# A convolution and attention-plus-scan kernel: the projection's convolution spread over the whole step, halo rows kept in one tile, and GpSimd's output products taken in pairs

## The chip, the cores and the metric

One NeuronCore of a Trainium2 chip runs the whole program. The metric is device time in microseconds for one execution. The kernel before took 16,462.36 us, the median of three runs (16,461.45 to 16,478.73 us).

## What is computed

The input `x` is 2 images of 256 x 256 positions with 128 channels, in fp32. Two layers follow, each with a residual and each on a group-normalised input `_gn` (32 groups of 4 channels, statistics over the whole image).

Layer 0 is an attention along one image axis. It takes some 15% of the time and the change does not touch it.

Layer 1 is a state-space layer. Cut to what matters:

```python
xi, z = split(x @ in_proj_w.T)               # 256 channels each
xi = silu(depthwise_conv3x3(xi) + conv_b)    # over the image
xs = xi.reshape(B, 256, L)                   # L = 65536 positions
dts, Bs, Cs = split(x_proj_w @ xs)           # 8, 16 and 16 rows
delta = softplus(dt_w @ dts + dt_b)          # 256 x L
# for every channel d (256) and state n (16), along L:
h = exp(delta * A[d, n]) * h + delta * xs * Bs[n]
y[d] = sum_n Cs[n] * h[d, n] + Ds[d] * xs[d]
y = layernorm(y) * silu(z)
out = x + y @ out_proj_w.T
```

The recurrence is sequential over the 65,536 positions of an image, for 256 x 16 = 4,096 pairs of a channel and a state.

## The kernel before

**Tiling.** Layer 1 goes through each image in steps of R = 4 rows, T = 1,024 positions: 64 steps an image, 128 in all. In a step the 4,096 pairs of channel and state are NU = 32 *units* of 128 partitions each, a partition being one channel with one of SR = 4 states of a group. A unit's number t gives the step k, the half of the channels h (2), the group of states m (4) and the quarter q of the half (4), in that order, q fastest (`unit`, line 907).

**What a unit is.** Five operations on tiles of 128 x 1024:
- `drive` (line 948, GpSimd): hb = du x B, from two tiles that DMA has replicated, `du_r` and `bb`
- `decay` (line 940, ScalarE): da = exp(delta x A), into PSUM. There are two da tiles, for even and for odd units
- `scan` (line 954, VectorE): the recurrence. For most units it writes its result over da; for a *pooled* unit over hb
- `product` (line 966): yc = h x C, from the replicated tile `cc`. VectorE does it, for pooled units GpSimd (line 970)
- `remember` (line 961, ScalarE): keeps the last column as the state for the next step

`add_up` (line 975, TensorE) then sums the products of four units into y, in 8 matmuls (16 records in the profile). At h's first group it starts y with Ds x xs (line 984). `pooled` (line 937) names 9 of 32 units by their number in the step: `POOLED = (4, 7, 10, 13, 16, 19, 24, 26, 31)`.

**What else a step holds.** `project(k)` (line 606) makes what step k needs: rows loaded and turned (`load`, `turn`), normalised into `xn` (`normalise`), the convolution as nine matmuls with shifted views for each of four output blocks (`conv`, two records a matmul in the profile), z (`gate`), then x_proj (`states`), dt_w (`size`), softplus and du = delta x xs (`times`, GpSimd). Three long ScalarE operations belong to it: `silu_xs`, `softplus`, `silu_z`, each 128 x 2048, each with a table of its own, so that a table is loaded ahead of it and exp's again ahead of the next decay. Its convolution needs a halo: the last two rows of xn are kept by GpSimd in a tile `keep` and copied into the next xn by GpSimd. All the projection's matmul results go through one PSUM buffer, tag "p": one must be evacuated by ScalarE before the next begins. `finish_row` (line 804) does the layernorm, gate and output projection for a row of the step before, nine pieces in nine slots; its `gated` (line 872) is a VectorE product of 128 x 512. Its results go through one PSUM buffer too, tag "f".

**The order.** It is written out by hand for TensorE, ScalarE, VectorE and GpSimd (`manual_schedule`, line 1017): one slot for each unit. In slot t the program issues, in this order, `drive(t + 2)`, the GpSimd product of unit t - 1 if pooled, `decay(t + 1)`, `scan(t)` and VectorE's product of t, `add_up` for units t - 5 to t - 2 if t - 5 is a multiple of four, then the pieces of projections and rows that `at(slot, piece)` has put into the slot, in the order of their entry, and at last `remember(t)`. Each engine runs its part of that list in order. In a projection of step k the slots count from `base` = 32 (k - 2), so it runs one to two steps ahead: convolution and z in slots 2 to 18 after base, silu_xs in 21, states and sizes in 22 to 28, softplus in 29, times in 31 and 32, silu_z in 33. DMAs are issued from SyncE, whose order is not written out; `fetch(t + 6)` (line 916) asks for a unit's replicated tiles six slots ahead. `bb` and `cc` have three buffers, `delta_r` and `du_r` five each.

Of the kernel before, what the change touches and what calls it, by code (L numbers as in the profile page):

```python
# [8 lines left out]
F32 = mybir.dt.float32  # L9
AF = mybir.ActivationFunctionType  # L10
ALU = mybir.AluOpType
# [4 lines left out]
P = 128  # L16
# [5 lines left out]
def attn_then_ssm_kernel(  # L22
# [557 lines left out]
    NU = NCG * NSG  # L580
    NM = NQ * NSG

    POOLED = (4, 7, 10, 13, 16, 19, 24, 26, 31)
    s1 = ctx.enter_context(tc.tile_pool(name="s1", bufs=1))
    s2 = ctx.enter_context(tc.tile_pool(name="s2", bufs=2))
    s3 = ctx.enter_context(tc.tile_pool(name="s3", bufs=3))
    s5 = ctx.enter_context(tc.tile_pool(name="s5", bufs=5))
    s8 = ctx.enter_context(tc.tile_pool(name="s8", bufs=8))
    ps_d = ctx.enter_context(tc.tile_pool(name="ps_d", bufs=1, space=PSUM))
    ps_y = ctx.enter_context(tc.tile_pool(name="ps_y", bufs=1, space=PSUM))  # L590
    ps_p = ctx.enter_context(tc.tile_pool(name="ps_p", bufs=1, space=PSUM))
# [5 lines left out]

    slots = {}

    def at(t, piece, *args):  # L600
        slots.setdefault(t, []).append((piece, args))

    halo = {}
    given = {}

    def project(k):
# [19 lines left out]
                )  # L626

        def begin():


            xn = o["xn"] = s1.tile([P, R + 2, WP], F32, name="xn")
            nc.gpsimd.memset(xn[:, :, 0:1], 0.0)
            nc.gpsimd.memset(xn[:, :, WP - 1 : WP], 0.0)
            if s == 0:
                nc.gpsimd.memset(xn[:, 0, :], 0.0)
                turn("first", 0, 1)
                normalise(1, 1)
            else:
                nc.gpsimd.tensor_copy(xn[:, 0:2, 1 : W + 1], halo.pop(k - 1))
            if n < R:  # L640
                nc.gpsimd.memset(xn[:, 2 + n, :], 0.0)

        def turn(src, r, m):
            t_ps = o["t"] = ps_p.tile([P, RB, W], F32, name="t_ps", tag="p")
# [5 lines left out]

        def normalise(to, m):
            nc.scalar.activation(
                o["xn"][:, to : to + m, 1 : W + 1],
                o["t"][:, 0:m, :],
                AF.Identity,
                bias=sh,
                scale=rs,
            )

        def keep():  # L660
            if s + 1 < NSTEP:
                halo[k] = s2.tile([P, 2, W], F32, name="keep")
                nc.gpsimd.tensor_copy(halo[k], o["xn"][:, R : R + 2, 1 : W + 1])

        def conv(h, i, dy):
            if dy == 0:
                o["u"] = ps_p.tile([P, RB, W], F32, name="u_ps", tag="p")
            for dx in range(3):
                nc.tensor.matmul(  # L669
                    o["u"],  # L670
                    w_tap[:, h, 3 * dy + dx, :],
                    o["xn"][:, i * RB + dy : i * RB + dy + RB, dx : dx + W],
                    start=(dy == 0 and dx == 0),
                    stop=(dy == 2 and dx == 2),
                )

        def conv_out(h, i):
            if (h, i) == (0, 0):
                o["xs"] = s1.tile([P, NH, T], F32, name="xs")
            nc.scalar.activation(  # L680
                o["xs"][:, h, i * TB : (i + 1) * TB],
                o["u"].rearrange("p r w -> p (r w)"),
                AF.Identity,
                bias=cb_c[:, h : h + 1],
            )
# [6 lines left out]
        def gate(h, i):  # L692
            o["z"] = ps_p.tile([P, RB, W], F32, name="z_ps", tag="p")
            nc.tensor.matmul(
                o["z"],
                w_z[:, h, :],
                o["xn"][:, 1 + i * RB : 1 + (i + 1) * RB, 1 : W + 1],
                start=True,
                stop=True,
            )  # L700
# [62 lines left out]
            nc.gpsimd.tensor_tensor(du, o["delta"][:, h, :], du, ALU.mult)  # L763
            nc.sync.dma_start(out=v["du"][h], in_=du)

        at(base - 14, load)
        at(base - 4, begin)
        for r in range(0, n, RB):
            at(base - 3 + r, turn, "raw", r, min(RB, n - r))
            at(base - 2 + r, normalise, 2 + r, min(RB, n - r))  # L770
        at(base + 1, keep)
        t = base + 2
        for h in range(NH):
            for i in range(NB):
                for dy in range(3):
                    at(t + dy, conv, h, i, dy)
                at(t + 3, conv_out, h, i)
                at(t + 3, gate, h, i)
                at(t + 4, gate_out, h, i)
                t += 4  # L780
        t = base + 21
        at(t, silu_xs)
        at(t + 1, states, 0)
        at(t + 2, states_out, 0)
        at(t + 2, states, 1)
        at(t + 3, states_out, 1)
        t += 3
        for h in range(NH):
            for i in range(NB):
                at(t, size, h, i)  # L790
                at(t + 1, size_out, h, i)
                t += 1
        at(base + 29, softplus)
        at(base + 31, times, 0)
        at(base + NU, times, 1)
        at(base + NU + 1, silu_z)

    def finish(k):

        b, s = steps[k]  # L800
        for r in range(R):
            finish_row(k, b, R * s + r, r * W, (k + 1) * NU + 3 + r * (NU // R))

    def finish_row(k, b, row, t0, a):
        o = {}

        def fetch():
            o["xres"] = s2.tile([P, WT, C], F32, name="xres")
            nc.sync.dma_start(
                out=o["xres"], in_=x1[b][row].rearrange("(t p) c -> p t c", p=P)  # L810
            )
            o["szr"] = s2.tile([P, NH, W], F32, name="szr")
            nc.sync.dma_start(
                out=o["szr"], in_=given[k]["sz"][:, :, t0 : t0 + W].rearrange("h p t -> p h t")
            )
# [78 lines left out]
                in_=ob,  # L894
            )

        at(a - 3, fetch)
        for i, piece in enumerate(
            (turn, stats, scales, norm, back, affine, gated, mix, leave)
        ):  # L900
            at(a + i, piece)

    states_of = {}
    ys = {}
# [2 lines left out]
    def unit(t):  # L907

        k, i = divmod(t, NU)
        h, i = divmod(i, NM)  # L910
        m, q = divmod(i, NQ)
        return k, h, m, q
# [3 lines left out]
    def fetch(t):  # L916
        k, h, m, q = unit(t)
        v = given[k]
        if q == 0:

            for name, row in (("bb", m * SR), ("cc", NS + m * SR)):
                tl = repeats[name, k, h, m] = s3.tile([P, T], F32, name=name)
                nc.sync.dma_start(
                    out=tl, in_=v["bc"][row : row + SR, :].partition_broadcast(CQ)
                )
        if m == 0:

            for name in ("delta", "du"):
                tl = spreads[name, k, h, q] = s5.tile([P, T], F32, name=f"{name}_r")
                nc.sync.dma_start(  # L930
                    out=tl,
                    in_=v[name][h, q * CQ : (q + 1) * CQ, :]
                    .unsqueeze(1)
                    .to_broadcast([CQ, SR, T]),
                )

    def pooled(t):
        return t % NU in POOLED

    def decay(t):  # L940
        k, h, m, q = unit(t)
# [4 lines left out]
        )  # L946

    def drive(t):
        k, h, m, q = unit(t)
        hb = s5.tile([P, T], F32, name="hb")  # L950
        units[t] = {"hb": hb}
        nc.gpsimd.tensor_tensor(hb, spreads["du", k, h, q], repeats["bb", k, h, m], ALU.mult)  # L952

    def scan(t):
        k, h, m, q = unit(t)
# [10 lines left out]
    def product(t):  # L966
        k, h, m, q = unit(t)
        u = units[t]
        u["yc"] = s8.tile([P, T], F32, name="yc")
        eng = nc.gpsimd if pooled(t) else nc.vector  # L970
        eng.tensor_tensor(u["yc"], u["h"], repeats["cc", k, h, m], ALU.mult)  # L971

    outs = {}

# [26 lines left out]
    def y_out(t):  # L1001
        k, h, _, _ = unit(t)
        ys[k, h] = s2.tile([P, T], F32, name=f"ys{h}")
        nc.scalar.copy(ys[k, h], outs["y"])
# [12 lines left out]
    with tc.manual_schedule(engines=engines):  # L1017
        for t in range(min(slots), max(slots) + 1):
            if 0 <= t + AHEAD < end:
                fetch(t + AHEAD)  # L1020
            if 0 <= t < end and t % (NU * NSTEP) == 0:
                st = s1.tile([P, NCG, NSG], F32, name="state")
                nc.gpsimd.memset(st, 0.0)
                states_of[steps[t // NU][0]] = st
            if 0 <= t + 2 < end:
                drive(t + 2)
            if 0 <= t - 1 < end and pooled(t - 1):
                product(t - 1)
            if 0 <= t + 1 < end:
                decay(t + 1)  # L1030
            if 0 <= t < end:
                scan(t)
                if not pooled(t):
                    product(t)
            if 0 <= t - 5 < end and (t - 5) % NQ == 0:
                add_up(t - 5)
            if 0 <= t - 6 < end and unit(t - 6)[2:] == (NSG - 1, 0):
                y_out(t - 6)
            for piece, args in slots.pop(t, ()):
                piece(*args)  # L1040
            if 0 <= t < end:
                remember(t)

# [36 lines left out]
```

## Time and profile before

| | |
|---|---|
| median of three runs | 16,462.36 us |
| the profiled execution | 16,465.48 us |
| its span, first to last instruction | 16,463.4 us |
| first scan starts | 2,690.5 us into the span |
| last scan ends | 16,405.2 us |
| the 128 steps between | 13,714.6 us, 107.15 us each |

The profile's page gives, engine by engine, the busy time and its share, and then the costliest groups of instructions: the source line, the engine, the operation, output and input tiles with partitions x elements, the count, the busy time in us, the mean of one instruction in ns, and the idle time of that engine just ahead of them with what ended it. A timeline has the start in us, the length in us, engine, line, operation and tiles, and in brackets the idle time ahead of it with its releaser. PE is TensorE, DVE VectorE, ACT ScalarE, POOL GpSimd, SP SyncE. Consecutive instructions of an engine overlap a little where neither waits, so the cost of one is the distance between starts.

### The profile page before, as it was taken

The page shows a single profiled execution, that of the slowest core. Times are in us where ns is not written, and L with a number is a line of the kernel's source. Part 1 is how long each engine was busy: PE and PEld are TensorE (multiplying, and loading weights), DVE is VectorE, ACT ScalarE, POOL GpSimd, SP SyncE. Part 2 cuts the span into 40 slices and gives each one's busy share as a digit, 9 for nine tenths or more (in the row PEclk, how much of TensorE's full clock was granted, in tenths as well). Part 3 has the DMA queues.
Part 4 walks back from the last instruction along what each step waited for, and adds up shares of the span by engine and source line. Part 5 has one row for each costly group of instructions (what it writes and reads, how often), then busy time and mean ns, then how long its engine had stood idle before and what let it go on. Part 6 is the DMA issues. An engine that isn't in the chain of part 4 may idle for free. (4 is left out here: it accounts for less than half of the span.)

```text
span 16463.4 us, 177150 instructions
## 1 busy us (share of the span) xinstructions
PE 13687.6 (83%) x55353; PEld 6810.9 (41%) x55353; DVE 14807.3 (90%) x12607; ACT 11039.0 (67%) x19870; POOL 13686.2 (83%) x7308
## 2 busy tenths in 40 slices
PE   6999997888888888888888888888888888888886
PEld 5777873333333333333333333333333333333333
DVE  7665555999999999999999999999999999999998
ACT  3555554677776677766777766777776767777665
POOL 0111114999999999999999999999999999999998
PEclk9999998888899888889998889999889998889997
DMA  4322224666666666666666666666666666666665
GB/s 186 131 86 88 82 83 146 232 234 230 232 234 230 233 232 232 233 229 232 233 233 231 233 228 232 232 235 231 230 229 230 234 234 231 233 230 234 230 231 171
DMA packets 1428932, 3452.05 MB, mean 210 GB/s; under 512 B 119784, under 2 KB 711184, under 8 KB 1407504
## 3 DMA queue, kind: packets, MB, share of 16 engines
q1 hardware_dynamic: 1427984, 3440.73, 60.6%
q8 instruction: 434, 7.11, 0.2%
q14 instruction: 514, 4.21, 0.1%
HBM read 2752.41 MB, written 687.88 MB: 209 GB/s over the span
## 5 line engine op out<-in xcount | busy, mean ns | idle before, releaser
L952 POOL TENSOR_TENSOR hb<-du_r,bb 128x1024 f32<-128x1024 f32 x4096 | 9575.1, 2363 | 0.0
L959 DVE TENSOR_TENSOR_SCAN da<-da,state,hb 128x1024 f32<-128x1024 f32 x2944 | 6903.2, 2345 | 327.8 <-ACT da L944 321.8
L944 ACT ACTIVATE da<-delta_r,a_neg 128x1024 f32<-128x1024 f32 x4096 | 4576.8, 1117 | 88.6 <-ACT state L964 0.8
L669 PE MATMUL u_ps<-xn,w_tap 128*128 128x512 f32 x9216 | 4230.3, 604 | 181.8 <-ACT state L964 168.2
L971 DVE TENSOR_TENSOR yc<-da,cc 128x1024 f32<-128x1024 f32 x2944 | 3604.7, 1224 | 254.9 <-DVE da L959 5.0
L971 POOL TENSOR_TENSOR yc<-hb,cc 128x1024 f32<-128x1024 f32 x1152 | 2719.6, 2361 | 203.0 <-issue 166.6
L959 DVE TENSOR_TENSOR_SCAN hb<-da,state,hb 128x1024 f32<-128x1024 f32 x1152 | 2697.3, 2341 | 72.6 <-ACT da L944 72.5
L991 PE MATMUL y<-yc,sel 128*32 128x512 f32 x16384 | 2527.4, 682 | 236.6 <-POOL yc L971 229.9
L669 PEld LDWEIGHTS u_ps<-xn,w_tap 128*128 128x128 f32 x9216 | 1718.3, 193 | 2190.5 <-issue 1781.4
L428 POOL TENSOR_TENSOR x1g<-xc,bo_all 128x512 f32<-128x512 f32 x256 | 315.9, 1273 | 1841.6 <-DVE stats L477 1839.7
L964 ACT COPY state<-da 128x1 f32<-128x1 f32 x2944 | 459.6, 156 | 1527.6 <-DVE yc L971 1525.8
L991 PEld LDWEIGHTS y<-yc,sel 128*32 128x32 f32 x16384 | 496.8, 116 | 1937.6 <-issue 1117.5
L821 PE MATMUL yt<-centre,ys 128*128 128x256 f32 x4096 | 1072.2, 407 | 218.4 <-ACT ob L891 217.4
L680 ACT ACTIVATE xs<-u_ps,cb_c 128x512 f32<-128x512 f32 x512 | 351.9, 687 | 1257.3 <-PE u_ps L669 977.9
L856 PE MATMUL yd<-ident,yn 128*128 128x128 f32 x2048 | 403.4, 331 | 906.5 <-ACT yn L845 877.5
L378 ACT ACTIVATE e<-s_ps,nmx 128x256 f32<-128x256 f32 x1024 | 477.6, 476 | 967.3 <-DVE nmx L369 955.1
L717 PE MATMUL xd_ps<-xs,w_xp 128*64 128x512 f32 x1024 | 683.5, 805 | 479.6 <-ACT state L964 374.8
L821 PEld LDWEIGHTS yt<-centre,ys 128*128 128x128 f32 x4096 | 794.2, 200 | 602.7 <-ACT ob L891 379.2
L735 PE MATMUL dt_ps<-xd,w_dt 8*128 8x512 f32 x1024 | 693.6, 761 | 270.7 <-ACT xd L730 263.9
L856 PEld LDWEIGHTS yd<-ident,yn 128*128 128x128 f32 x2048 | 291.2, 169 | 1263.8 <-ACT yn L845 916.2
L345 DVE TENSOR_TENSOR v<-v_ps,bv_all 128x512 f32<-128x512 f32 x256 | 177.0, 691 | 592.0 <-PE v_ps L338 592.0
L881 PEld LDWEIGHTS o_ps<-w_out,yg 128*128 128x128 f32 x4096 | 626.8, 219 | 41.4
(131 smaller groups left out, 17289.1 us busy)
## 6 DMA issues: line engine op xcount, KB each, us to landing
bb<-bc_d SPq DMA_DIRECT2D x1024, 512.0 KB, 4.2
cc<-bc_d SPq DMA_DIRECT2D x1024, 512.0 KB, 5.3
delta_r<-delta_d SPq DMA_DIRECT2D x1024, 512.0 KB, 5.6
du_r<-du_d SPq DMA_DIRECT2D x1024, 512.0 KB, 4.1
xs_d<-xs SPq DMA_DIRECT2D x128, 1024.0 KB, 6.9
xr<-xs_d SPq DMA_DIRECT2D x256, 512.0 KB, 7.2
delta_d<-delta SPq DMA_DIRECT2D x128, 1024.0 KB, 6.9
du_d<-xs SPq DMA_DIRECT2D x256, 512.0 KB, 3.2
```

Source lines behind the costliest of these rows:

```text
L378: nc.scalar.activation(e[:, i, :], o["s", r][:, i, :], AF.Exp, bias=o["nmx", r][:, i : i + 1], scale=SM, accum_out=o["den"][:, r, i : i + 1],)
L669: nc.tensor.matmul(o["u"], w_tap[:, h, 3 * dy + dx, :], o["xn"][:, i * RB + dy : i * RB + dy + RB, dx : dx + W], start=(dy == 0 and dx == ...
L717: nc.tensor.matmul(o["xd_ps"], w_xp[:, h, :], o["xs"][:, h, i * TB : (i + 1) * TB], start=(h == 0), stop=(h == NH - 1),)
L735: nc.tensor.matmul(o["dt"], w_dt[:, h, :], o["xd"][0:DR, i * TB : (i + 1) * TB], start=True, stop=True,)
L821: nc.tensor.matmul(o["yt"][:, j, :], ys[k, h][:, t0 + j * P : t0 + (j + 1) * P], centre[:, (1 - h) * P : (1 - h) * P + DI], start=(h == 0) ...
L856: nc.tensor.transpose(o["yd"][:, h, j * P : (j + 1) * P], o["yn"][:, j, h * P : (h + 1) * P], ident,)
L881: nc.tensor.matmul(o["o"][:, j, :], o["yg"][:, h, j * P : (j + 1) * P], w_out[:, h, :], start=False, stop=(j == WT - 1 and h == NH - 1),)
L944: nc.scalar.activation(da, spreads["delta", k, h, q], AF.Exp, scale=a_neg[:, g, m : m + 1])
L952: nc.gpsimd.tensor_tensor(hb, spreads["du", k, h, q], repeats["bb", k, h, m], ALU.mult)
L959: nc.vector.tensor_tensor_scan(u["h"], u["da"], u["hb"], st, ALU.mult, ALU.add)
L971: eng.tensor_tensor(u["yc"], u["h"], repeats["cc", k, h, m], ALU.mult)
L991: nc.tensor.matmul(y[q * CQ : (q + 1) * CQ, cols], sel, units[t + q]["yc"][:, cols], start=False, stop=(m == NSG - 1),)
```

## The change

- **Pooled units come in pairs.** `POOLED = (6, 10, 14, 22, 30)` names even units; each stands for itself and the next: 10 of 32. GpSimd's product is one instruction over both (128 x 2 x 1024), with `cc` broadcast over the pair, in the slot after the second unit.
- **`drive` works by pairs for all units**: one GpSimd instruction in each odd slot t, for units t + 3 and t + 4, with `bb` broadcast over the pair. `hb` has three pair buffers (before: five single ones), `du_r` three pair buffers (five single ones), `yc` four pair buffers (eight single ones).
- `bb` and `cc` have two buffers in place of three; `xs` has two in place of one; `xres` and `szr` one in place of two, asked for one slot ahead of the row's first piece in place of three.
- **One `xn` tile stays for the whole layer.** It is zeroed once; ScalarE copies its last two rows to its first two at a step's beginning. GpSimd's two edge memsets, `keep` and the copy back go.
- **The convolution is spread**: its four blocks begin in slots 3, 11, 19 and 27 after base, with 2, 2, 3 and 2 of the nine taps in the block's slots 0, 1, 2 and 4, and are evacuated in slot 5 of the block. z goes to slots 2, 24, 25 and 26; silu_z to 29, silu_xs to 37, states to 40 and 41, sizes to 42, 48, 49 and 50, softplus to 53, times to 55 and 56. In the numbers of the running step silu_xs stands in slot 5, softplus in 21, silu_z in 29.
- Rows begin in slot 7 of the step in place of 3, so VectorE's `gated` falls into slots 5, 13, 21 and 29 (before: 1, 9, 17, 25). `add_up` and `y_out` come one slot later.
- In a slot, pieces without TensorE work are issued ahead of those with it.

```diff
-    POOLED = (4, 7, 10, 13, 16, 19, 24, 26, 31)
+    POOLED = (6, 10, 14, 22, 30)
...
+    xn = s1.tile([P, R + 2, WP], F32, name="xn")
+    nc.gpsimd.memset(xn, 0.0)
...
-                nc.gpsimd.tensor_copy(xn[:, 0:2, 1 : W + 1], halo.pop(k - 1))
+                nc.scalar.copy(xn[:, 0:2, 1 : W + 1], xn[:, R : R + 2, 1 : W + 1])
...
+        CY = NU // 4
+        for c in range(4):
+            h, i = divmod(c, NB)
+            t = base + c * CY + 3
+            for dt, taps in ((0, (0, 1)), (1, (2, 3)), (2, (4, 5, 6)), (4, (7, 8))):
+                at(t + dt, conv, h, i, taps, pe=True)
+            at(t + 5, conv_out, h, i)
+        for t, (h, i) in ((2, (0, 0)), (24, (0, 1)), (25, (1, 0)), (26, (1, 1))):
+            at(base + t, gate, h, i, pe=True)
+            at(base + t + 1, gate_out, h, i)
+        at(base + 29, silu_z)
+        at(base + 37, silu_xs)
+        for t, i in ((40, 0), (41, 1)):
+            at(base + t, states, i, pe=True)
+            at(base + t + 1, states_out, i)
+        for t, (h, i) in ((42, (0, 0)), (48, (1, 0)), (49, (0, 1)), (50, (1, 1))):
+            at(base + t, size, h, i, pe=True)
+            at(base + t + 1, size_out, h, i)
+        at(base + 53, softplus)
+        at(base + 55, times, 0)
+        at(base + 56, times, 1)
...
-                tl = repeats[name, k, h, m] = s3.tile([P, T], F32, name=name)
+                tl = repeats[name, k, h, m] = s2.tile([P, T], F32, name=name)
...
     def pooled(t):
-        return t % NU in POOLED
+        return t % NU - t % 2 in POOLED
...
     def drive(t):
+
         k, h, m, q = unit(t)
-        hb = s5.tile([P, T], F32, name="hb")
-        units[t] = {"hb": hb}
-        nc.gpsimd.tensor_tensor(hb, spreads["du", k, h, q], repeats["bb", k, h, m], ALU.mult)
+        hb = s3.tile([P, 2, T], F32, name="hb")
+        units[t] = {"pair": hb, "hb": hb[:, 0, :]}
+        units[t + 1] = {"hb": hb[:, 1, :]}
+        nc.gpsimd.tensor_tensor(
+            hb,
+            spreads["pair", k, h, q],
+            repeats["bb", k, h, m].unsqueeze(1).to_broadcast([P, 2, T]),
+            ALU.mult,
+        )
...
+    def products(t):
+
+        k, h, m, q = unit(t)
+        hb = units[t]["pair"]
+        yc = s4.tile([P, 2, T], F32, name="yc")
+        for i in range(2):
+            units[t + i]["yc"] = yc[:, i, :]
+        nc.gpsimd.tensor_tensor(
+            yc, hb, repeats["cc", k, h, m].unsqueeze(1).to_broadcast([P, 2, T]), ALU.mult
+        )
...
-            if 0 <= t + 2 < end:
-                drive(t + 2)
-            if 0 <= t - 1 < end and pooled(t - 1):
-                product(t - 1)
+            if 0 <= t + 3 < end and t % 2:
+                drive(t + 3)
+            if 0 <= t - 2 < end and t % 2 == 0 and pooled(t - 2):
+                products(t - 2)
...
-            if 0 <= t - 5 < end and (t - 5) % NQ == 0:
-                add_up(t - 5)
+            if 0 <= t - 6 < end and (t - 6) % NQ == 0:
+                add_up(t - 6)
```

## The prediction

> **What bounds the kernel now.** I read the page's shares and costliest groups first, then the waits of VectorE, the starts of all 4,096 scans in VectorE's timeline, and then two steps closely.
>
> ```profile
> PE 13687.6 (83%) x55353; PEld 6810.9 (41%) x55353; DVE 14807.3 (90%) x12607; ACT 11039.0 (67%) x19870; POOL 13686.2 (83%) x7308
> L952 POOL TENSOR_TENSOR hb<-du_r,bb 128x1024 f32<-128x1024 f32 x4096 | 9575.1, 2363 | 0.0
> L959 DVE TENSOR_TENSOR_SCAN da<-da,state,hb 128x1024 f32<-128x1024 f32 x2944 | 6903.2, 2345 | 327.8 <-ACT da L944 321.8
> L971 DVE TENSOR_TENSOR yc<-da,cc 128x1024 f32<-128x1024 f32 x2944 | 3604.7, 1224 | 254.9 <-DVE da L959 5.0
> L971 POOL TENSOR_TENSOR yc<-hb,cc 128x1024 f32<-128x1024 f32 x1152 | 2719.6, 2361 | 203.0 <-issue 166.6
> ```
>
> Two engines are nearly full at once. The shares are over the whole span; the windows view of a short step, the first here, gives VectorE 97% and GpSimd 98%; the second is a long one:
>
> ```profile
> 8044.57:8150.84 106.27, 86.32 (x330) 37.46 (x329) 103.09 (x59) 75.35 (x129) 104.41 (x56) 0.92 0.67 233
> 5898.66:6010.14 111.48, 93.13 (x330) 41.08 (x330) 103.47 (x60) 75.39 (x129) 106.31 (x57) 0.85 0.68 233
> ```
>
> Columns: length, then busy us of PE, PEld, DVE, ACT, POOL, then TensorE's granted clock. Between starts of scans a unit on VectorE alone costs 3.57 us, a pooled one 2.26, and `gated` adds 0.60. So 23 x 3.573 + 9 x 2.26 + 4 x 0.60 = 104.9 us a step if VectorE never waited. Most steps take 105.7 to 106.4, about one in four 109 to 112; the mean is 107.15.
>
> The missing 2.2 us are waits for da:
>
> ```profile
> DVE da L959 <- ACT da L944: 321.8, 317, 148.8
> DVE hb L959 <- ACT da L944: 72.5, 38, 2.4
> ```
>
> Less the 148.8 us ahead of the first scan it is 246 us, 1.9 a step. By unit: 33 us at unit 0 and 67 at unit 8 (0.3 and 0.5 in nearly each step), and 150 in units 28 to 31, of the long steps alone. There TensorE is the culprit. The same pair of size records, in a short and in a long step:
>
> ```profile
> 8135.36 1.12 PE L735 MATMUL dt_ps<-xd,w_dt 8*128 8x512 f32 x2
> ...
> 5992.59 2.07 PE L735 MATMUL dt_ps<-xd,w_dt 8*128 8x512 f32 x2
> ```
>
> In slots 21 to 31 there is no convolution; TensorE waits some 3 us for silu and states, and in a long step then runs at half speed for some 17 us. `size_out` waits for it, decay queues behind that, and VectorE loses 4 to 6 us.
>
> **What the Trainium skill says.** "TensorE: Matmul & The Clock Gate", Part 1, has the array at half clock after an idle window of about 3.4 us, and at full clock after such a window of sustained work. The 1.12 and 2.07 us agree in size, and the waits ahead (3.1 us in the long step) are near that length. "GPSIMD Engine Reference", section 1, names contention with VectorE where its instruction has two SBUF inputs. The scan and the product have one input in PSUM, and hb and pooled products take 2.363 and 2.361 us alike, so I charge none. "ScalarE: Activation LUTs", What ACT_TABLE_LOAD costs, gives 1,283 ns; the trace has 1.28 each, and the next activation starts at once.
>
> **Part 1: a tenth pooled unit.** VectorE's step becomes 22 x 3.573 + 10 x 2.26 + 4 x 0.60 = 103.6 us, 1.31 less; x 128 = -168 us.
>
> **Part 2: GpSimd's bill.** Back to back its products start 2.31 us apart:
>
> ```profile
> 8053.77 9.31 POOL L952 TENSOR_TENSOR hb<-du_r,bb 128x1024 f32<-128x1024 f32 x4
> ```
>
> Before: 32 + 9 + 2 = 43 of them, 99.3 us, four row scales at 1.07 (lve to the next product), and memsets and copies 1.4: 105.0, all that a step has. After: 16 + 5 paired, two single (4.6), scales 4.3. A paired product isn't in the trace. Bounds: twice 2.31 = 4.62 if nothing is saved; a tenth above that if the broadcast operand costs something. Layer 0's product with two broadcast dimensions takes 1.272 us for 512 elements; with 2.363 for 1,024 this extrapolates to 4.54 busy for 2,048. The skill's GPSIMD page, 3.1, has 4,497 ns. Less the 0.05 overlap, 4.45 to 4.49; I take 4.47. Sum: 21 x 4.47 + 8.9 = 102.8 us, below VectorE's.
>
> The order must hold too. With three hb pairs, the product of units 6 and 7 can start only after scan 7, and until unit 28's drive GpSimd then has 13 paired products, two scales and two `times`: 13 x 4.47 + 2.1 + 4.6 = 64.8 us after scan 7's end. VectorE needs in the same stretch (end of scan 7 to start of unit 28, with the waits of part 4) 65.4. Unit 16 is similarly close. So 0.5 us of slack, nothing lost; at 4.62 it would be 1.4 us a step late.
>
> **Part 3: waits that go.** With taps in most slots TensorE's longest gap by the new order is about 2.7 us (evacuations in slot 3), so I expect the half-speed stretches to go, and with them 150 us. Unit 8's wait (norm and gate_out in 6 and 7 ahead of a decay) and unit 0's also go: slots 6 and 7 now hold only a leave. Together -246 us, 1.92 a step. The convolution itself costs the same 72 records.
>
> **Part 4: a wait that comes.** The softplus slot in the trace, ScalarE's lines and then VectorE's:
>
> ```profile
> 8141.31 1.12 ACT L944 ACTIVATE da<-delta_r,a_neg 128x1024 f32<-128x1024 f32 x1
> 8142.44 1.28 ACT L754 ACT_TABLE_LOAD   x1
> 8143.74 1.91 ACT L754 ACTIVATE delta<-delta 128x2048 f32<-128x2048 f32 x1
> 8145.56 0.14 ACT L964 COPY state<-da 128x1 f32<-128x1 f32 x1
> 8145.71 1.28 ACT L944 ACT_TABLE_LOAD   x1
> 8147.01 1.12 ACT L944 ACTIVATE da<-delta_r,a_neg 128x1024 f32<-128x1024 f32 x1
> ```
>
> ```profile
> 8141.00 2.35 DVE L959 TENSOR_TENSOR_SCAN da<-da,state,hb 128x1024 f32<-128x1024 f32 x1
> 8144.59 2.35 DVE L959 TENSOR_TENSOR_SCAN da<-da,state,hb 128x1024 f32<-128x1024 f32 x1
> 8148.23 2.35 DVE L959 TENSOR_TENSOR_SCAN hb<-da,state,hb 128x1024 f32<-128x1024 f32 x1
> ```
>
> The decay of unit t + 2 ends 7.13 us after scan t starts, and scan t + 2 begins at 7.2. It is hidden because units t and t + 1 are both VectorE's, 3.6 us each. In the new order all three long operations stand in slots 5, 21 and 29, each with `gated` behind it and a pooled pair next: scan t + 2 could start after 3.59 + 0.60 + 2.26 = 6.45 us but must wait until 7.21. That is 0.76 us three times, 2.28 a step, +292 us. Behind the late decay are the next decays, which have the following 3.6 us unit to recover.
>
> **Part 5: the smaller edits.** ScalarE's halo copy (0.6 us like z's copy) falls in slot 0, behind conv_out and a row's stats: 1.43 + 1.1 + 0.7 + 0.6 against 3.6, and decay 2 has another 3.6, so nothing; without that cover 0.6 us a step. GpSimd's own 1.4 us are in part 2. SyncE's volume of DMA is unchanged. With two `cc` buffers the tile for units 16 to 19 can be asked for only after the product of units 10 and 11, and lands 5.3 us later (median of cc). From scan 7's end GpSimd needs for that p(6,7), two drives, a scale and p(10,11): 19.0 us; plus 5.3 = 24.3. VectorE wants it after 26.2. I charge nothing and keep 0 to 2 us a step for the range. `xs`, `xres` and `szr` have most of a step or a row (26 us) for transfers of 4 to 7. `times` moves from 33 slots ahead of its step to nine, six ahead of the first drive that wants du; the du store and load between (3.2 + 4.1 us) have some 18 us.
>
> **The ends.** Before the first scan the old order runs two whole projections (148.8 us); the new one reaches the first decay without the second's last block, silu_xs, states and sizes: from 2,655 to 2,689 us in the trace, less a gate and silu_z, about -25. The last product by pairs adds 2.
>
> **Sum**, against the profiled execution of 16,465.5 us (span 16,463.4 and 2.1 around it): -168 - 246 + 292 - 25 + 2 = -145, so 16,320. The median lies 3 us below that execution: **16,317 us**, a step of 106.2.
>
> **Rivals.**
> 1. *The silu wait is covered*, since something lets the decays start earlier. For: ScalarE is only 67% busy. Against: the decay needs the da tile that a VectorE unit frees at the slot's start. Then VectorE asks 103.6 and GpSimd 102.8, with its order at about 104: (104.0 - 107.15) x 128 - 23 for the ends - 3 = -429, **16,036 us**.
> 2. *TensorE stays cold.* Spread work leaves it gaps in each slot, and at half speed nine taps take 16 us of their 18 us window; conv_out then holds decays as sizes do now. For: it waits for evacuation of one buffer all along. Against: no gap reaches 3 us by the order. The 1.92 us come back half or more: about **16,450 us**.
> 3. *GpSimd becomes the bound* (slower). If a paired product starts 4.77 us apart (3% above two single ones), the stretch of part 2 takes 68.8 us against 65.4, 3.4 us a step: 106.2 + 3.4 - 107.15 = 2.45, x 128 - 26 (ends and median) = +288: **16,750 us**. It decides from about 4.60, where 1.1 us late in each step uses up the gain. For: GpSimd has no slack now; against: 1.272 us for a broadcast one.
> 4. *`cc` comes late*: SyncE, which issues in its own order, has a wait for a row in front of it. 1.7 us at unit 16: 107.9 a step, **16,530 us**.
>
> **How the numbers follow.** Chances: forecast 0.55, rival 1 0.10, rival 2 0.13, rival 3 0.10, rival 4 0.12. A difference under 0.2% (33 us) can't be told from none here. Faster: 0.55 + 0.10 + a third of rival 2, and I keep 0.70; same 0.10; slower 0.20. The forecast's own range, with a pair of 4.40 to 4.60 and `cc` at 0 to 1 us, is 16,230 to 16,420. For eight in ten I reach down half-way to rival 1 and up to rival 4: 16,150 to 16,540.
>
> **What would show it.** Part 1: 22 of 32 products on VectorE. Part 2: the mean of the paired products, near 4.5 us, and no wait of a scan for hb. Part 3: granted clock above 0.92, no size records of 2.07. Part 4: waits for da of some 0.76 us at units 7, 23 and 31, and hardly elsewhere. I am wrong if scans wait for hb or VectorE's products for `cc`, or if those three waits aren't there.

## The result, and the profile after

The changed kernel takes 17,059.0 us (median of four runs, 17,051.8 to 17,063.0) against 16,461.9 us for the kernel before (16,449.4 to 16,478.7). The ratio is 1.0362, 95% interval 1.0344 to 1.0379. It is slower; the forecast was a gain of 0.9%, and the time lies above its range.

The page of the changed kernel, its shares and the groups that answer to those shown of before, with one group more, ScalarE's `norm`:

```profile
PE 13889.4 (81%) x55353; PEld 6834.6 (40%) x55353; DVE 14710.5 (86%) x12479; ACT 11084.3 (65%) x19997; POOL 13476.9 (79%) x4240
L954 POOL TENSOR_TENSOR hb<-du_r,bb 128x2048 f32<-128x2048 f32 x2048 | 9252.8, 4534 | 732.0 <-DMA du_r<-du_d 665.5
L966 DVE TENSOR_TENSOR_SCAN da<-da,state,hb 128x1024 f32<-128x1024 f32 x2816 | 6610.4, 2347 | 868.9 <-ACT da L944 744.4
L980 DVE TENSOR_TENSOR yc<-da,cc 128x1024 f32<-128x1024 f32 x2816 | 3447.6, 1224 | 183.7 <-DVE da L966 1.8
L966 DVE TENSOR_TENSOR_SCAN hb<-da,state,hb 128x1024 f32<-128x1024 f32 x1280 | 2981.1, 2342 | 289.7 <-ACT da L944 288.2
L989 POOL TENSOR_TENSOR yc<-hb,cc 128x2048 f32<-128x2048 f32 x640 | 2899.9, 4531 | 391.7 <-DVE hb L966 254.9
L838 ACT ACTIVATE yn<-yt,rstd 128x256 f32<-128x256 f32 x1024 | 430.0, 471 | 1772.8 <-POOL rstd L834 1772.8
```

Every engine's share of the span fell: nothing became full. VectorE does 97 us less work and GpSimd 209 us less, in a span 594 us longer. So the time went into waits. VectorE still waits for da alone, now 1,033 us of it:

```profile
DVE da L966 <- ACT da L944: 744.4, 584, 3.9
DVE hb L966 <- ACT da L944: 288.2, 458, 1.3
```

The columns are us in all, times, and the longest. Before it was 246 us in the steps. The sum closes: with the few us of waits for others, scans wait 1,035 us now and waited 251 before, +784; the tenth pooled unit takes 168 off by the forecast's own sum, the first scan, at 2,661.6 us, comes 29 earlier, and what follows the last scan takes 4 longer: +591, against spans of 17,057.8 and 16,463.4 us, +594.

By unit, over the 128 steps: 268 us at units 7, 23 and 31, the three waits of part 4. The other 767 were not foreseen, nearly all of them 220 at unit 4, 20 at units 10 and 11, 140 at unit 12, 249 at unit 20, 91 at units 25 and 26, 45 at unit 28. They lie close behind the places where ScalarE sits idle, and the group of line 838 above says for what: `norm` waits 1,773 us for `rstd`, a tile of 128 x 2 that GpSimd makes. Before, it waited 4.5 us in the whole run:

```profile
L845 ACT ACTIVATE yn<-yt,rstd 128x256 f32<-128x256 f32 x1024 | 421.0, 461 | 4.5 <-POOL rstd L841 4.3
```

The waits at units 4, 12, 20 and 28 come directly behind a late `norm`. Those at 25 and 26 lie behind pieces of ScalarE that wait for TensorE, first of all `leave` (line 884) for the output rows of a row whose `norm` came late; with the row scales in time, in e1 below, they are gone too. The start of one step, in the timelines of GpSimd, ScalarE and VectorE:

```profile
8485.73 4.53 POOL L954 TENSOR_TENSOR hb<-du_r,bb 128x2048 f32<-128x2048 f32 x1 [4.89 <-DMA du_r<-du_d]
8490.20 4.55 POOL L989 TENSOR_TENSOR yc<-hb,cc 128x2048 f32<-128x2048 f32 x1
8494.83 4.53 POOL L954 TENSOR_TENSOR hb<-du_r,bb 128x2048 f32<-128x2048 f32 x1
8499.45 0.19 POOL L833 TENSOR_SCALAR lve<-lss 128x2 f32<-128x2 f32 x1
8499.72 0.69 POOL L834 TENSOR_TENSOR rstd<-lve,neg_half 128x2 f32<-128x2 f32 x1
```

```profile
8494.94 1.12 ACT L944 ACTIVATE da<-delta_r,a_neg 128x1024 f32<-128x1024 f32 x1
8500.44 0.84 ACT L838 ACTIVATE yn<-yt,rstd 128x256 f32<-128x256 f32 x2 [4.39 <-POOL rstd L834]
8501.17 0.78 ACT L652 ACTIVATE xn<-t_ps,sh,rs 128x512 f32<-128x512 f32 x1
8501.84 0.17 ACT L971 COPY state<-da 128x1 f32<-128x1 f32 x1
8502.03 1.12 ACT L944 ACTIVATE da<-delta_r,a_neg 128x1024 f32<-128x1024 f32 x1
```

```profile
8498.22 2.35 DVE L966 TENSOR_TENSOR_SCAN da<-da,state,hb 128x1024 f32<-128x1024 f32 x1
8500.60 1.22 DVE L980 TENSOR_TENSOR yc<-da,cc 128x1024 f32<-128x1024 f32 x1
8503.25 2.36 DVE L966 TENSOR_TENSOR_SCAN da<-da,state,hb 128x1024 f32<-128x1024 f32 x1 [1.43 <-ACT da L944]
```

The statistics of the row were ready at 8,489.6 (ScalarE's line 826). The row scale (lines 833 and 834, 0.9 us of work) stands in GpSimd's queue behind a paired product and a paired drive, so `rstd` comes at 8,500.4. ScalarE stands at `norm` from 8,496.1 on, with a load's evacuation, a state and a decay queued behind it; that decay ends at 8,503.15 and the scan starts then.

The row scales are programmed in slots 1, 9, 17 and 25 and start, in units that VectorE has reached, at 3.3, 11.0, 19.3 and 27.0 on average: two slots late. A drive for three slots ahead may run that late with no scan noticing it, and no scan of the changed kernel waits for hb. In the kernel before (drives two slots ahead) the scales were less than one slot late and `norm` found them done.

The chain above begins with another wait, 665 us in all in the page: GpSimd's drive for units 2 and 3 waits 5.2 us in every step for du. SyncE's queue ahead of it:

```profile
8474.44 0.51 SPq L930 DMA_DIRECT2D delta_r<-delta_d  x1
8475.00 0.60 SPq L916 DMA_DIRECT2D cc<-bc_d  x1
8476.48 0.51 SPq L930 DMA_DIRECT2D delta_r<-delta_d  x1
8477.09 0.55 SPq L930 DMA_DIRECT2D du_r<-du_d  x1
8479.56 0.51 SPq L930 DMA_DIRECT2D delta_r<-delta_d  x1
8480.13 0.60 SPq L930 DMA_DIRECT2D du_r<-du_d  x1
```

The pair's buffer came free at 8,470.8, when the drive that read it ended. But the two halves of du are each asked for behind a load of delta, which waits for a decay to free its buffer. The second half leaves at 8,480.1 and the drive starts 5.6 us later.

### The profile page after: what moved, and what is told of

Its sections match the earlier page's. It is cut to its first block, busy times and chain, and to the rows that moved or that the text cites. A ratio compares the mean times of both kernels' runs of the same rounds, so it can differ in the third digit from the quotient of the medians.

```text
span 17057.8 us, 170595 instructions
## 1 busy us (share of the span) xinstructions
PE 13889.4 (81%) x55353; PEld 6834.6 (40%) x55353; DVE 14710.5 (86%) x12479; ACT 11084.3 (65%) x19997; POOL 13476.9 (79%) x4240
## 5 line engine op out<-in xcount | busy, mean ns | idle before, releaser
L954 POOL TENSOR_TENSOR hb<-du_r,bb 128x2048 f32<-128x2048 f32 x2048 | 9252.8, 4534 | 732.0 <-DMA du_r<-du_d 665.5
L966 DVE TENSOR_TENSOR_SCAN da<-da,state,hb 128x1024 f32<-128x1024 f32 x2816 | 6610.4, 2347 | 868.9 <-ACT da L944 744.4
L665 PE MATMUL u_ps<-xn,w_tap 128*128 128x512 f32 x9216 | 4558.0, 643 | 57.8 <-ACT delta L742 27.3
L980 DVE TENSOR_TENSOR yc<-da,cc 128x1024 f32<-128x1024 f32 x2816 | 3447.6, 1224 | 183.7 <-DVE da L966 1.8
L966 DVE TENSOR_TENSOR_SCAN hb<-da,state,hb 128x1024 f32<-128x1024 f32 x1280 | 2981.1, 2342 | 289.7 <-ACT da L944 288.2
L989 POOL TENSOR_TENSOR yc<-hb,cc 128x2048 f32<-128x2048 f32 x640 | 2899.9, 4531 | 391.7 <-DVE hb L966 254.9
L690 PE MATMUL z_ps<-xn,w_z 128*128 128x512 f32 x1024 | 706.6, 777 | 1092.3 <-ACT state L971 1079.3
L838 ACT ACTIVATE yn<-yt,rstd 128x256 f32<-128x256 f32 x1024 | 430.0, 471 | 1772.8 <-POOL rstd L834 1772.8
L690 PEld LDWEIGHTS z_ps<-xn,w_z 128*128 128x128 f32 x1024 | 177.6, 217 | 1558.4 <-ACT state L971 1515.1
L759 POOL TENSOR_TENSOR xs<-delta,xs 128x1024 f32<-128x1024 f32 x256 | 606.1, 2368 | 95.3 <-ACT delta L750 95.3
```

The lines of the kernel that those rows point to most:

```text
L665: nc.tensor.matmul(o["u"], w_tap[:, h, tap, :], xn[:, i * RB + dy : i * RB + dy + RB, dx : dx + W], start=(tap == 0), stop=(tap == 8),)
L690: nc.tensor.matmul(o["z"], w_z[:, h, :], xn[:, 1 + i * RB : 1 + (i + 1) * RB, 1 : W + 1], start=True, stop=True,)
L954: nc.gpsimd.tensor_tensor(hb, spreads["pair", k, h, q], repeats["bb", k, h, m].unsqueeze(1).to_broadcast([P, 2, T]), ALU.mult,)
L966: nc.vector.tensor_tensor_scan(u["h"], u["da"], u["hb"], st, ALU.mult, ALU.add)
L980: nc.vector.tensor_tensor(u["yc"], u["h"], repeats["cc", k, h, m], ALU.mult)
L989: nc.gpsimd.tensor_tensor(yc, hb, repeats["cc", k, h, m].unsqueeze(1).to_broadcast([P, 2, T]), ALU.mult)
```

## The experiments

Theory A: the order of GpSimd's queue, the row scales behind a paired drive, makes `norm` and so decays late. Theory B: the late du on SyncE is the cause. Theory C: the three long ScalarE operations ahead of pooled pairs are, which the forecast had priced. All times are medians, and ratios are to the kernel before, with a 95% interval. The runs were made in three sessions on three chips, in which the kernel before took 16,461 us (e1 to e4), 16,443 (e5 to e7) and 16,456 (e8, e9); a difference in us between runs of two sessions is sure to some 20 us.

### The two repairs, apart and together

`e1_scales`: the row scale one slot earlier, in the slot of the statistics.

```diff
-        for i, piece in enumerate(
-            (turn, stats, scales, norm, back, affine, gated, mix, leave)
+        for i, piece in (
+            (0, turn), (1, stats), (1, scales), (3, norm), (4, back),
+            (5, affine), (6, gated), (7, mix), (8, leave),
```

> The changed kernel with one edit: a row's scales on GpSimd are issued one slot earlier, in the slot of its stats, so ahead of the paired drive of the next odd slot and not behind it. Theory A (queue order): the 1.77 ms in which ScalarE's norm waits for rstd are the cause; decays queue behind norm, and VectorE's waits at units 4, 12, 20, 26 and 28 (745 us in all) go, unless GpSimd's 5.2 us wait for du a step then sets the pace: 16,310 to 16,650 us. Theory B (late du): GpSimd is late because it idles for du_r once a step, and where the scales stand in its queue matters little: 16,850 to 17,060 us. Theory C (the three long ScalarE operations ahead of pooled pairs, 268 us, with the rest following from them): no change, 17,000 to 17,100 us.

`e2_du`: du asked for two slots ahead of delta. `fetch_row` is the part of `fetch` that asks for one tile of delta or du.

```diff
+            if 0 <= t + AHEAD + 2 < end:
+                fetch_row(t + AHEAD + 2, "du")
```

> The changed kernel with one edit: the du tiles of a half are asked for two slots ahead of its delta tiles, so that in SyncE's order du no longer stands behind delta loads that wait for a decay. Theory A: GpSimd's 665 us of waiting for du go, but scales still stand behind a paired drive; norm keeps waiting at units 12, 20 and 26 and less at 4: 16,800 to 17,050 us. Theory B: GpSimd gains 5.2 us a step, is in time for the scales, and the waits behind norm go: 16,310 to 16,550 us. Theory C: no change.

`e3_both`: both edits.

> The changed kernel with both edits: scales one slot earlier, du asked for two slots earlier. Theories A and B, and any mix of them: the step comes to the 106.2 us of the forecast, 16,300 to 16,420 us, with waits for da left only at units 7, 23 and 31 (0.7 us each). If it stays above 16,550 us, something else holds the decays.

| | us | ratio |
|---|---|---|
| e1_scales | 16,460.7 | 0.9996 (0.9987 to 1.0005) |
| e2_du | 16,824.2 | 1.0220 (1.0205 to 1.0235) |
| e3_both | 16,418.1 | 0.9975 (0.9965 to 0.9985) |

One pair of GpSimd instructions a row, moved by one slot, gives back 598 us, all of what was lost. The waits of e1 in VectorE and ScalarE:

```profile
DVE hb L967 <- ACT da L945: 267.1, 379, 1.3
DVE da L967 <- POOL hb L955: 160.7, 317, 1.1
```

```profile
ACT yn L838 <- POOL rstd L834: 295.3, 222, 2.8
```

The first line is the three predicted waits, and is nearly all that is left of the waits for da. In e2 the waits for du fall to 42 us, the wait at unit 4 is gone (220 us; the time falls by 235), and the waits at 12, 20 and 26 stand:

```profile
DVE da L972 <- ACT da L950: 552.4, 460, 2.3
DVE hb L972 <- ACT da L950: 267.1, 379, 1.3
```

```profile
ACT yn L838 <- POOL rstd L834: 1520.1, 512, 5.4
```

So A holds and is the larger: without its cure 1,520 us of `norm`'s waits remain. B is a second, smaller cause that acts through A: in e1 GpSimd still waits 402 us for du, and unit 4 waits 22 us in all. Repaired after A it is worth 43 us. C explains its 268 us and no more.

In e3 a step is 107.02 us; less the waits of scans it is 103.65, as forecast (103.6). The main waits:

```profile
DVE hb L973 <- ACT da L951: 267.2, 379, 1.3
DVE da L973 <- POOL hb L961: 137.0, 287, 0.9
```

The second line is at units 28 (106 us), 16 and 20, where VectorE now waits for GpSimd. Between scan 7 and unit 28, in GpSimd's and VectorE's timelines:

```profile
8143.79 4.53 POOL L996 TENSOR_TENSOR yc<-hb,cc 128x2048 f32<-128x2048 f32 x1 [2.67 <-DVE hb L973]
...
8202.37 0.19 POOL L833 TENSOR_SCALAR lve<-lss 128x2 f32<-128x2 f32 x1
...
8205.62 13.52 POOL L961 TENSOR_TENSOR hb<-du_r,bb 128x2048 f32<-128x2048 f32 x3
```

```profile
8141.21 2.35 DVE L973 TENSOR_TENSOR_SCAN hb<-da,state,hb 128x1024 f32<-128x1024 f32 x1 [0.70 <-ACT da L951]
...
8210.19 2.36 DVE L973 TENSOR_TENSOR_SCAN da<-da,state,hb 128x1024 f32<-128x1024 f32 x1 [0.86 <-POOL hb L961]
```

GpSimd takes 66.3 us from 8,143.8 to the end of the first of those three drives, and VectorE would have come after 65.5. The forecast had 64.8 with two row scales in the stretch. Scales issued a slot earlier stand in slots 8, 16 and 24, and the last, 0.9 us at 8,202.4, now comes ahead of unit 28's drive of slot 25. Without it the sum is 65.4, so in this step the repair uses up what slack there was.

### Which half of the pairing

`e4_single`: the changed kernel with one drive per unit, for unit t + 2 as before; products stay paired.

```diff
...
-            if 0 <= t + 3 < end and t % 2:
-                drive(t + 3)
+            if 0 <= t + 2 < end:
+                drive(t + 2)
```

> The changed kernel with drives by single units again, issued for unit t + 2 in slot t as before the change; the tiles are the same pairs and the pooled products stay paired. GpSimd has 16 x (2 x 2.31 - 4.48) = 2.2 us more to do in a step. Theory A: the scales of a slot stand at most two units' drives ahead of the scan in place of four, so norm waits less and the kernel gets faster in spite of that work: 16,500 to 16,850 us. Theory B: more work for an engine that idles for du: 17,050 to 17,350 us.

`e5_spread`: the spread convolution, halo and rows of the changed kernel, and all of GpSimd's pairing undone (drives, products, the list of nine units, buffers of hb, du and yc).

```diff
-    POOLED = (6, 10, 14, 22, 30)
+    POOLED = (4, 7, 10, 13, 16, 19, 24, 26, 31)
...
-            if 0 <= t + 3 < end and t % 2:
-                drive(t + 3)
-            if 0 <= t - 2 < end and t % 2 == 0 and pooled(t - 2):
-                products(t - 2)
+            if 0 <= t + 2 < end:
+                drive(t + 2)
+            if 0 <= t - 1 < end and pooled(t - 1):
+                product(t - 1)
```

> One part alone: convolution and projections in the changed kernel's slots, rows, add_up, xn and buffers of bb, cc, xs as changed, but GpSimd's work by single units as before (drive for t + 2, nine pooled units of the old list, five hb and du buffers, eight yc). Theory A (GpSimd's queue ahead of the row scales): VectorE asks 104.9 us a step, GpSimd 103.8, no long ScalarE operation stands ahead of a pooled unit within two; if scales stay in time as in the kernel before, 105.3 a step, 16,200 to 16,300 us; if norm waits for rstd as with single drives in the changed kernel (6.9 us a step there), 16,350 to 16,550 us. If the spread itself were at fault for the slowdown: 16,700 us and more.

`e9_pairdrive`: e5 with paired drives for t + 3 and their buffers; products stay single.

```diff
...
-            if 0 <= t + 2 < end:
-                drive(t + 2)
+            if 0 <= t + 3 < end and t % 2:
+                drive(t + 3)
```

> The spread alone (16,245 us) with one part of the pairing added: drives by pairs, issued in odd slots for units t + 3 and t + 4, three pair buffers for hb and du; products by single units, nine pooled as before. GpSimd's work falls by 2.2 us a step. Theory A (row scales stand behind a paired drive, norm waits, decays queue behind it): slower all the same, by about what single drives gave back in the changed kernel (438 us): 16,550 to 16,750 us, with norm's waits for rstd near 1 to 1.5 ms. If the loss needs the paired products too: 16,150 to 16,300 us.

With the changed kernel they fill a table, all on the spread convolution:

| | products single, 9 units | products paired, 10 units |
|---|---|---|
| drives single, t + 2 | e5: 16,245.0 (0.9864 to 0.9897) | e4: 16,620.7 (1.0082 to 1.0112) |
| drives paired, t + 3 | e9: 16,648.3 (1.0102 to 1.0132) | changed kernel: 17,059.0 (1.0344 to 1.0379) |

The spread alone, that is the whole change without GpSimd's pairing, is a gain of 1.2%. Paired drives cost 403 us beside single products and 438 beside paired ones, paired products (with the tenth pooled unit) 376 and 411. Both make `norm` wait for the row scales, as ScalarE's waits in e5, e9 and e4 show, in that order:

```profile
ACT yn L838 <- POOL rstd L834: 137.0, 121, 2.7
```

```profile
ACT yn L838 <- POOL rstd L834: 983.2, 385, 6.7
```

```profile
ACT yn L838 <- POOL rstd L834: 880.7, 263, 4.4
```

But that is not all of their cost. In e9 VectorE waits 426 us for da, 266 us of it at unit 4 alone (in the first line):

```profile
DVE hb L965 <- ACT da L944: 300.3, 185, 3.5
DVE da L965 <- ACT da L944: 125.9, 338, 1.6
```

Just before, at unit 0, GpSimd's drive stands still for 6.2 us in every step and mostly starts within 0.2 us of the landing of a du tile. So the larger part of e9's loss looks like theory B's late request, which makes the row scale late behind it, as at unit 4 of the changed kernel, where e2 removed the wait. Of e4's waits only 151 us are for da at units 20, 25 and 26, where the changed kernel has them too; 291 us are waits like part 4's at units 7, 23 and 31, and 148 us are for hb. How e4's and e9's costs divide was not tried: e9 with du asked for earlier would tell. What the order of the row scales is worth is shown by e1, not by this table.

`e7_spread_scales`: e5 with the scales edit of e1.

> The kernel of the spread alone with the row scales one slot earlier. Theory A: whatever it loses to norm waiting for rstd goes: 105.2 us a step, 16,180 to 16,280 us, about VectorE's own sum. If it is no faster than the spread alone, rstd was in time there already.

It takes 16,364.7 us, 0.9953 (0.9939 to 0.9968), which is 120 us slower than e5 and misses what was expected. GpSimd and VectorE:

```profile
POOL lve L833 <- ACT yn L826: 359.3, 168, 11.1
```

```profile
DVE da L953 <- POOL hb L946: 153.7, 195, 1.2
```

With single drives GpSimd runs close to its program, so a scale in the slot of the statistics comes too early: GpSimd waits for them, and its drives come late. The same edit is worth -598 us on a queue that runs two slots late and +120 us on one that does not.

### The waits behind the long operations

`e6_pooled`: e3 with pooled pairs moved, so that none follows a slot with a long ScalarE operation.

```diff
-    POOLED = (6, 10, 14, 22, 30)
+    POOLED = (2, 10, 14, 18, 26)
```

> The kernel with both edits (scales a slot earlier, du two slots earlier) and the pooled pairs moved to units 2, 10, 14, 18 and 26, so that none follows a slot with silu_xs, softplus or silu_z. If the 268 us of waits at units 7, 23 and 31 come from those operations, they go and nothing like them appears: 103.7 to 105 us a step, 16,000 to 16,200 us, with GpSimd (102.8 us a step) perhaps holding scans by some tenths. If the waits belong to pooled pairs as such, they move to units 3, 11, 15, 19 and 27 and the time stays at 16,400 us or grows.

It takes 16,563.6 us, 1.0073 (1.0058 to 1.0088). The three waits are gone and no new pair has one, so part 4's cause is shown; but the time did not fall to the 16,000 to 16,200 us expected, it rose by some 150. VectorE and GpSimd:

```profile
DVE da L973 <- POOL hb L961: 557.6, 364, 3.9
DVE yc L987 <- DMA cc<-bc_d: 46.0, 73, 2.8
```

```profile
POOL hb L961 <- DMA bb<-bc_d: 385.2, 122, 5.0
```

The new wait is for bb, nearly all of it for that of units 4 to 7. On SyncE its request leaves behind that for `cc` of units 0 to 3, which waits until GpSimd's product of units 26 and 27 frees a buffer, and then behind one load of du, three of delta and a store.

`e8_bb`: e6 with bb asked for two slots earlier. `fetch_group` is the part of `fetch` that asks for bb or `cc`.

```diff
+                fetch_group(t + AHEAD + 2, "bb", unit(t + AHEAD + 2)[2] * SR)
```

> The kernel with pooled pairs at 2, 10, 14, 18 and 26 (16,564 us) with bb asked for two slots earlier, so that in SyncE's order fewer cc loads, which wait for a pooled product, stand in front of it. If its waits for hb at units 4, 20 and 28 come from GpSimd's 385 us of waiting for bb, most go: 16,150 to 16,350 us. If they come from GpSimd's own order (three hb pairs, in-order products), they stay: 16,450 to 16,570 us.

```profile
DVE da L977 <- POOL hb L965: 296.7, 245, 1.9
DVE da L977 <- ACT da L955: 8.0, 18, 1.3
```

It takes 16,236.5 us, 0.9868 (0.9852 to 0.9885), inside the range expected, with no waits for bb left and almost none for da. The expectation had bb pass loads of `cc`. In the trace bb of units 4 to 7 still leaves behind the same `cc`, but ahead of two delta loads and the store, 2.0 us after `cc` in place of 4.1. The wait for hb at unit 4 (194 us) is gone, that at unit 20 fell from 157 to 72 us, and that at unit 28 stayed (207 and 224), 2.3 us a step for both. There GpSimd is the bound: from unit 8 to that drive it works without a pause. At unit 8 it stood still for 0.8 us a step until a row's statistics were ready, which is a price of the early scale, as in e7. The whole change, with three orders mended and the pooled pairs moved, stands where the spread alone stands (16,245.0); the two are not told apart.

## Why the prediction was wrong

**Part 1, the tenth pooled unit: right.** e3's step less its waits is 103.65 us.

**Part 2, the price of a paired product: right.** Busy 4.53 us, 4.48 to 4.50 between starts, against 4.47. The Trainium skill, "GPSIMD Engine Reference", 3.1, has 4,497 ns; the trace has 4,534 busy. GpSimd's sum of 102.8 us a step was met too.

**Part 2, the order: the step that failed.** The forecast charged "four row scales at 1.07" as GpSimd's time, tested its order only against hb ("end of scan 7 to start of unit 28"), and wrote "So 0.5 us of slack, nothing lost". It did not ask who waits for the row scale, and so put the path from the scale through `norm` and the decays to the scans at nothing; it measured 1,773 us of `norm`'s waits and nearly all of 767 us of VectorE's. `norm` is programmed one slot behind the scale, a paired drive is 4.5 us, and drives for three slots ahead let GpSimd run two slots behind its program without harm to any scan; only the small instruction between them has a reader that soon. e1 moves it one slot and the 598 us are back. For hb itself the count was not contradicted: VectorE waits for none in the changed kernel, though that one is nearly 6 us a step slower than forecast, and e3's wait at unit 28 comes with a third row scale in the stretch.

**Part 3, waits that go: right where the row scales are in time, but not altogether for the reason given.** e1 and e3 have no waits for da left at units 0, 8 and 28 to 30, and e5 has no wait left at units 0, 8 and 28 to 31: 96 us in all, 65 of them new ones at unit 2. In the changed kernel the granted clock is 0.912, not above 0.92, and a size record takes 802 ns on average against 761 before; in e1, with the same spread, it is 0.948 and 724 ns. So more of TensorE's time at half speed in the changed kernel was an effect of the late engines ahead of it. The forecast had expected the half-speed stretches to go, and they did not altogether: of 1,024 size records 152 still take over 1 us in e5, against 234 before. Scans no longer wait behind them.

**Part 4, three silu waits: right in place, cause and size.** 0.70 us each at units 7, 23 and 31, 268 us in all against 292, and gone in e6.

**Part 5, the small edits: one failed.** Of du the forecast said that store and load "have some 18 us". The data did have the time. What was late was the request: with pairs, two halves must arrive, each behind a delta load on SyncE. It is worth 235 us alone and 43 after the scales. `cc` cost nothing in the changed kernel; in e6, with other pairs, it waits for a paired product and holds up bb behind it, which is part of GpSimd's 385 us there.

**The ends: right**, 29 us earlier against 25, and 4 us later against 2.

**The rivals.** None was what happened. The silu waits were not covered (1); TensorE is not cold by the spread itself (2); the pair's price is 4.49, below the 4.60 from which GpSimd was to bound (3); no scan's product waits for `cc` (4). The slower case named a price, where the loss was in an order. With both orders mended the kernel takes 16,418 us, 101 above the forecast and inside its range; the 137 us of waits for hb cover that.

**Open:** three buffers for bb and `cc` beside the pairs, a row scale on another engine, and e9 with an earlier du were not tried.

## What to carry to other kernels

Here an engine that is nearly full ran two slots late, as its furthest deadline let it. A longer look-ahead or a longer instruction can so make every small instruction in its queue late by as much: for each small result on such an engine, ask who reads it, how soon, and what stands behind that reader. Price a merged instruction by its length in the queue, not only by its own cost, and follow each load through its own queue, where it leaves behind the load ahead of it and not when its buffer comes free. Where a change has two parts, run each alone: here the one gave 1.2% and the other took some 5% with it.

## What the runs showed that was not expected

- A tile of 128 x 2, 0.9 us of work a row, made late by a slot or two, cost 598 of 17,059 us, while no engine was busy for over 86% of the span.
- The same one-slot edit is worth -598 us on the changed kernel and +120 us on the one with single drives.
- One GpSimd product of 128 x 2,048 with `bb` broadcast over the pair takes 4,534 ns, less than two of 128 x 1,024 without (2,363 each). What the broadcast alone costs is not known: no run has the long product without it.
- SyncE's order alone, one tile asked for two slots earlier (bb in e8), was worth some 330 us, with the same volume moved.
